# A chunked TTT scan and an FFN on one core: the scan's step planned in branches, its state in one PSUM tile, the weight guard on GpSimd

## The chip, the cores and the metric

The kernel runs on one core of a Trainium2 chip. The metric is the device time of one execution in microseconds. Three executions of the kernel before took 1038.76, 1048.29 and 1051.76 us; their median is 1048.29 us. The profile is of a further execution.

Five engines appear in it: PE (TensorE, matmuls; PEld is its loading of weights), DVE (VectorE), ACT (ScalarE), POOL (GpSimd) and SP (SyncE, which here only issues DMAs). Each runs its own instructions in the order in which the program holds them, and waits on semaphores of the others.

## The reference, cut to what matters

The input is x, 2048 rows of 512. The first layer projects its normalised rows to q, k, v (16 heads of 32 columns) and beta, and runs a scan over chunks of 16 rows:

```python
def step(S, inp):
    qi, ki, vi, ei = inp
    kh = einsum('bchd,bhde->bche', ki, S)
    target = vi - ki
    mu, rstd = mean(kh), rsqrt(var(kh) + EPS)
    kh_hat = (kh - mu) * rstd
    gw = (w * kh_hat + b - target) * w
    v_new = (gw - mean(gw) - kh_hat * mean(gw * kh_hat)) * rstd
    A = where(tri, einsum('bchd,bshd->bhcs', qi, ki), 0) * ei
    qh = einsum('bchd,bhde->bche', qi, S) - einsum('bhcs,bshe->bche', A, v_new)
    o = qi + _ln(qh, w, b)
    S = S - einsum('bchd,bche->bhde', ki * ei, v_new)
    return (S, o)
```

There are 128 such steps, and each needs the state S of the one before. A gate, a norm and a projection by Wo follow. The second layer is an FFN with 512 to 1536 to 512 columns, whose three weights are rounded to float8 (e4m3fn, as float32 values) before use, so that values beyond 448 become NaN.

## The kernel before

**The parts.** The rows are worked in 16 blocks of 128, each of 8 steps. For each block `pre` normalises, turns and projects the rows, and lays k out in `kb` and, by way of DRAM, in `kr`; `gram` forms the products of k with the k of the step before; `pre_v` makes the target rows; `pre_sig` makes q and the gate; `scores` and `post` make the output of a block that the scan has left. `weights` rounds the FFN's weights in 36 parts of 128 x 512 while the scan runs: DVE makes a magic number m per value (L1067, L1070), POOL adds and subtracts it (L1074, L1076), ACT makes a guard that is 0, or NaN beyond 448 (L1080, L1082), and POOL adds it (L1087). The FFN starts when the scan has ended.

**One step of the scan** (`chain`), with the names that the prediction uses:

1. DVE: the first product (L901) and the second (L906) of kh with prepared rows, then sums over the columns (L929).
2. ACT: the state S is copied from PSUM, in two operations, one for each of the two banks `ups[0]` and `ups[1]` (L916). PE: kS, the next step's k times that S, into the bank of kh (L877).
3. ACT: a root (L933). DVE: the reciprocal iv (L936), y (L939), k1 (L943), k2 (L951), sk (L953), kk (L956), and the product m (L959).
4. ACT: u, two operations (L946), from a row and k1.
5. DVE: u plus m (L969), and vb (L972), the new values.
6. PE: Gv (L990) adds gram times vb to kh, which completes the next step's kh; and up (L1002) adds the step's k times vb to the state, in PSUM.

The state, the small numbers and u share two PSUM banks, each a tile of its own: `ups[0]` holds half the state and `nums` (iv, y, kk), `ups[1]` the other half and u:

```python
ups = [p_up.tile([P, D], F32, tag=f"up{j}", name=f"up{j}")[:, 0:128] for j in range(2)]
nums, u = ups[0], ups[1][:, 64:128].rearrange("p (r e) -> p r e", r=2)
```

What must wait for what is found by the framework from the tiles that an instruction reads and writes; the kernel states none of it.

**The order.** A planner written into the kernel (`Sched`) sets each engine's order when the program is built. All work is tasks that ask for an engine for so many microseconds. The planner always places the operation that can start first, by its own durations (the table `steps` for a step of the scan, `TENSOR` for PE, with a switch cost `SWITCH` and a preference `SAME` for work of the same array shape). Tasks marked `chain` announce when they will need each engine (`need`); other work goes in front only if it ends no later than that plus `SLACK`. On PE, matmuls whose result nobody reads (`spare`, 128 x 384, named "none") are placed where less than `SPARE` of work lies in the last 3.4 us, and a shorter filler goes into kh's bank ahead of Gv (L982). The whole step is one task, `chain`, which asks for its operations one after the other. At a block's border the wait for the next block's `kb` and its kS stand before the sum of step 5.

Of the kernel before, what the change touches and what calls it, by code (L numbers as in the profile page):

```python
# [9 lines left out]
F32 = mybir.dt.float32  # L10
F32R = mybir.dt.float32r
I32 = mybir.dt.int32
AF = mybir.ActivationFunctionType
ALU = mybir.AluOpType
# [47 lines left out]

SPARE, SPARE_OVER, SPARE_GAP = 1.3, 0.1, 0.3
SWITCH, SAME = 0.1, 0.25
TENSOR = {
# [27 lines left out]
class Sched:  # L95
# [2 lines left out]

    SLACK = {"PE": 0.3, "DVE": 0.3, "ACT": 0.35, "POOL": 0.0, "SP": 0.0}

    def __init__(self):
        self.engine = {"PE": 0.0, "DVE": 0.0, "ACT": 0.0, "POOL": 0.0, "SP": 0.0}
# [77 lines left out]
    def run(self):  # L182
        while True:
            self._settle()
            ops = [t for t in self.tasks if t["req"][0] == "op"]
            if not ops:
                assert not self.tasks, [t["gen"].__name__ for t in self.tasks]
                return
            need = {}
            for t in ops:  # L190
                if t["chain"]:
                    at = self._start(t)
                    need[t["req"][1]] = at
                    for eng, after in (t["req"][3] or {}).items():
                        need.setdefault(eng, at + after)
            best = None
            for eng in self.engine:
                mine = [(self._start(t), t) for t in ops if t["req"][1] == eng]
                fit = [
                    (s, t) for s, t in mine  # L200
                    if t["chain"] or eng not in need or s + self._us(t) <= need[eng] + self.SLACK[eng] + t["req"][6]
                ]
                fit = [(s, t) for s, t in fit if t["req"][5] != "spare" or self._spare(s, t, mine, need.get(eng))]
                if not fit:
                    continue
                first = min(s for s, _ in fit)
                s, t = min(((s, t) for s, t in fit if s <= first + 1e-9), key=lambda x: self._rank(x[1]))
                if best is None or s < best[0]:
                    best = (s, t)
            s, t = best  # L210
            eng, dur = t["req"][1], self._us(t)
            if eng == "PE":
                _, self.part, work = TENSOR[t["req"][5]]
                self.idle = s - self.engine[eng]
                self.array.append((s, work))
            else:
                self.table = t["req"][5] or self.table
            self.engine[eng] = s + dur
            self.now = max(self.now, s)
            t["ready"] = s + dur + t["req"][4]  # L220
            t["last"] = eng
            self._advance(t, t["ready"])
# [11 lines left out]
def kernel(  # L234
# [79 lines left out]
    with ExitStack() as st1:  # L314
# [63 lines left out]
        kh_bank = p_kh.tile([P, D], F32, tag="kh", name="kh")  # L378
        kh = kh_bank[:, 0 : 2 * DH].rearrange("p (r e) -> p r e", r=2)

        ups = [p_up.tile([P, D], F32, tag=f"up{j}", name=f"up{j}")[:, 0:128] for j in range(2)]

        nums, u = ups[0], ups[1][:, 64:128].rearrange("p (r e) -> p r e", r=2)
        iv, y = nums[:, 64:66], nums[:, 66:74].rearrange("p (s r) -> p s r", r=2)
# [58 lines left out]
        def norm_row(src, tag, newton=False):  # L443

            yield op("DVE", 0.73)
            st = small.tile([P, 6], F32, tag=tag + "st", name="st")
            nc.vector.bn_stats(st, src)
            yield op("DVE", 0.18)
            mv = small.tile([P, 2], F32, tag=tag + "mv", name="mv")
            nc.vector.bn_aggr(mv, st)  # L450
            if newton:
                r = yield from rsqrt_parts(mv[:, 1:2], [P, 1], 1.0, 1e-5, small, tag + "n")
            else:
                yield ("take", tables, 1)
                end = yield op("ACT", 0.3, table="sqrt")
                z = small.tile([P, 1], F32, tag=tag + "z", name="z")
                act(z, mv[:, 1:2], AF.Sqrt, bias=eps5)
                tables.put(end)
                yield op("DVE", 0.4)
                r = small.tile([P, 1], F32, tag=tag + "r", name="r")  # L460
                nc.vector.reciprocal(r, z)
            nb = small.tile([P, 1], F32, tag=tag + "nb", name="nb")
            stt(nb, mv[:, 0:1], -1.0, r, ALU.mult, ALU.mult)
            return r, nb
# [307 lines left out]
        def post(b):  # L772
# [76 lines left out]


        steps = [
            ("DVE", 0.4, 0.0), ("DVE", 0.33, 0.4), ("ACT", 0.42, 0.32), ("PE", "kS", 0.86), ("DVE", 0.47, 0.73),
            ("ACT", 0.28, 1.32), ("DVE", 0.2, 1.2), ("DVE", 0.2, 1.4), ("DVE", 0.2, 1.6), ("ACT", 0.8, 1.92),
            ("DVE", 0.2, 1.8), ("DVE", 0.2, 2.0), ("DVE", 0.2, 2.2), ("DVE", 0.33, 2.4), ("DVE", 0.26, 2.84),
            ("DVE", 0.23, 3.1), ("PE", "Gv", 3.45, 0.2), ("PE", "up", 3.8, 0.22),
# [3 lines left out]
        def chain_ops():  # L859
            out = []  # L860
            for n, (eng, us, at, *late) in enumerate(steps):
                need = {}
                for m in range(1, len(steps) + 1):
                    e, _, start, *_ = steps[(n + m) % len(steps)]
                    need.setdefault(e, start - at + (period if n + m >= len(steps) else 0.0))
                need.pop(eng, None)
                late = late[0] if late else 0.0
                if eng == "PE":
                    out.append(pe(us, need, late))
                else:  # L870
                    out.append(op(eng, us, need, late, "sqrt" if (eng, us) == ("ACT", 0.28) else None))
            return out

        def k_S(b, i, S, stop):
            for g in range(4):
                half = slice(64 * (g % 2), 64 * (g % 2) + 64)
                nc.tensor.matmul(  # L877
                    kh[half, g // 2, :], lhsT=kbs[b % 2][:, i, g, :], rhs=S[:, g, :], start=(g < 2), stop=stop and g > 1,
                )

        def chain():
            ops = chain_ops()
# [4 lines left out]
            for b in range(NB):  # L887
                if b >= 2:
                    yield ("wait", at_out[b - 2])
                for i in range(NC):  # L890
# [16 lines left out]
                        row[:, :, 6:8, 0:DH], kh.unsqueeze(2).to_broadcast([P, 2, 2, DH]), row[:, :, 3:5, 0:DH],  # L907
                        ALU.mult,
                    )
                    op_S = next(step)  # L910
                    if b or i:
                        yield ("at", t_up + HOP)
                        yield op_S
                        S = state.tile([P, 4, DH], F32, tag="S" if i else "S0", name="S")
                        for j in range(2):
                            nc.scalar.copy(S[:, j:4:2, :], ups[j][:, 0 : 2 * DH].rearrange("p (r e) -> p r e", r=2))  # L916
                    if i == 0:
                        data[b]["S"] = S
                    op_K = next(step)
                    if not end:  # L920
                        nb, ni = (b, i + 1) if i + 1 < NC else (b + 1, 0)
                        n2 = 2 * nb + ni // NHALF
                        if ni:
                            yield ("wait", ready[nb])
                            yield op_K
                            k_S(nb, ni, S, False)
                    yield ("at", t0)
                    t0 = yield next(step)
                    nc.vector.tensor_reduce(z[:, 0:4, :].rearrange("p s r -> p r s"), row[:, :, 4:8, :], AX.X, ALU.add)  # L929
                    t1 = yield next(step)  # L930

                    sk = small.tile([P, 2, 2], F32, tag="sk", name="sk")
                    act(sk[:, 0, :], z[:, 2, :], AF.Sqrt)  # L933
                    yield ("at", t0)
                    yield next(step)
                    nc.vector.reciprocal(iv, z[:, 2, :])  # L936
                    yield next(step)
# [3 lines left out]

                    k1 = small.tile([P, 2, 2], F32, tag="k1", name="k1")
                    stt(k1, z[:, 0:6:5, :], -1.0 / DH, y[:, 3:4, :].to_broadcast([P, 2, 2]), ALU.mult, ALU.mult)  # L943
                    t3 = yield next(step)
                    for r in range(2):
                        act(u[:, r, :], row[:, r, 4, 0:DH], AF.Identity, bias=k1[:, 0, r : r + 1], scale=k1[:, 1, r : r + 1])  # L946
                    yield ("at", max(t1 + HOP, t2))
                    yield next(step)

                    k2 = small.tile([P, 2], F32, tag="k2", name="k2")  # L950
# [9 lines left out]
                        m, row[:, :, 2:4, 0:DH],  # L960
                        kk.rearrange("p s r -> p r s").unsqueeze(3).to_broadcast([P, 2, 2, DH]), ALU.mult,
                    )
                    if not end and ni == 0:
                        yield ("wait", ready[nb])
                        yield pe("kS")
                        k_S(nb, ni, S, False)
                    yield ("at", max(t3 + HOP, t4))
                    yield next(step)
                    tt(u, m[:, :, 0, :], u, ALU.add)  # L969
                    t5 = yield next(step)  # L970
# [2 lines left out]
                    sched.add(give(b, i, vb), rank=-4)  # L973
                    if end:
                        break
                    yield ("wait", gram_in[n2])
                    t_kh = yield next(step)
                    work, idle = sched.array_work()
# [76 lines left out]
        def one_part(f, part, raw, loaded, before, marks):  # L1055
# [6 lines left out]
            yield ("at", loaded)  # L1062
            yield from turn(0)
            yield ("take", ms, 1)
            yield op("DVE", 0.6)
            m = rnd.tile([P, D], F32, tag="m", name="m")
            ts(m.bitcast(I32), raw.bitcast(I32), 0x7F800000, None, ALU.bitwise_and)  # L1067
            marks[0].set(0.0)
            yield op("DVE", 0.6)
            ts(m, m, 2.0**-6, 1.5 * 2.0**20, ALU.max, ALU.mult)  # L1070
            yield from turn(1)
            yield op("POOL", 1.35)
# [3 lines left out]
            gtt(v, v, m, ALU.subtract)  # L1076
            marks[1].set(0.0)

            yield op("ACT", 0.65)
            act(m, v, AF.Copy, scale=1.1 * 2.0**119)  # L1080
            yield op("ACT", 0.65)
            act(m, m, AF.Copy, scale=0.0)  # L1082
            yield from turn(2)
            yield ("take", ws, 1)
            end = yield op("POOL", 1.35)
# [304 lines left out]
```

## Time and profile before

| what | value |
| --- | --- |
| runs | 1038.76, 1048.29, 1051.76 us (median 1048.29) |
| the profiled execution's own time | 1042.52 us |
| its span, first to last instruction | 1040.7 us |
| granted TensorE clock, mean | 0.971 |
| first product of the scan, first and last | 45.7 and 728.8 us |
| PE "none" matmuls (L1021) | 125, 106.1 us busy |
| ACT u (L946) | 256 operations, 0.381 us each |
| ACT copies of the state (L916) | 254 operations, 0.214 us each |
| ACT guard (L1080, L1082) | 72 operations, 45.2 us |
| POOL busy | 513.4 us |

The span falls into 45.7 us up to the first step, 683 us of scan, and the rest, which is FFN with the last blocks' output beside it. A matmul of this kernel in float32 leaves two records, which is why PE's counts are twice the program's. In the lists "idle before" is the time that the engine stood still ahead of an operation, and the name behind the arrow is what ended it. A table by stage gives for each engine the busy time, with the number of records in brackets, and then the granted clock, the share of the DMA engines and GB/s.

### The profile page before, as it was taken

Reading aid. Unit: us, or ns where it says so; the run is one execution under the profiler, and the core shown is the slowest. Engines: PE = TensorE matmul, PEld = TensorE weight load, DVE = VectorE, ACT = ScalarE, POOL = GpSimd, SP = SyncE. Lnnn points to the kernel's source line nnn. Section 1 sums busy time; section 2 is a strip of 40 time slices with the busy share of each in tenths; the row PEclk is TensorE's granted clock in tenths of the full one; section 3 lists DMA queues with packets and bytes.
Section 4 is the critical chain, followed back from the end, with each engine's and each line's share of the span. In section 5 each row is a group of like instructions: output and inputs, shape, how many; then the busy total and the mean of one; then the engine's idle time right before and its main releaser. Section 6 shows DMA issues by size and latency. Waiting matters only on the chain.

```text
span 1040.7 us, 22812 instructions
## 1 busy us (share of the span) xinstructions
PE 977.6 (94%) x8150; PEld 651.2 (63%) x8150; DVE 681.2 (65%) x2291; ACT 535.4 (51%) x1373; POOL 513.4 (49%) x476
## 2 busy tenths in 40 slices
PE   4899999999998899999999999999799999999996
PEld 2456665656654565555656556556467888888885
DVE  3267777778688468777675757656565476665635
ACT  1556756666666456674665657654332232232223
POOL 4648578778467587668375887533420010010001
PEclk9999999999899999999999999999899999999998
DMA  9423323324223222222313232232204000010001
GB/s 294 132 57 83 92 53 80 69 76 104 69 49 85 67 44 70 65 70 64 72 30 83 67 78 70 49 92 66 74 1 182 1 31 11 1 41 0 11 31 41
DMA packets 139393, 69.08 MB, mean 66 GB/s; under 512 B 106640, under 2 KB 119056, under 8 KB 139280
## 3 DMA queue, kind: packets, MB, share of 16 engines
q1 hardware_dynamic: 138256, 66.35, 24.2%
q8 instruction: 65, 1.06, 0.5%
q0 software_dynamic: 272, 0.87, 0.3%
q10 hardware_dynamic: 752, 0.40, 0.2%
q14 instruction: 48, 0.39, 0.1%
HBM read 41.25 MB, written 26.35 MB: 65 GB/s over the span
## 4 chain that ended last, share of the span: by engine, by line
PE 74%; DVE 11%; ACT 6%; DMA 3%; POOL 3%; issue 2%; SPq 0%; ACTq 0%; DVEq 0%; POOLq 0%
PE gu L1189 17%; PE acc L1218 8%; PE pk L487 5%; PE none L1021 5%; PE po L487 5%; PE pq L708 5%; PE up L1002 5%; PE pv L487 5%; PE kh L990 4%; PE kh L877 3%; PE pr L570 3%; PE pt L472 2%; ACT up L946 2%; DMA wv_s<-in_wv_dram 1%; PE qh L792 1%
## 5 line engine op out<-in xcount | busy, mean ns | idle before, releaser
L1189 PE MATMUL gu<-xh,w 128*128 128x512 f32 x384 | 152.4, 397 | 2.8 <-DVE sg L1237 2.1
L1189 PE MATMUL gu<-xl,w 128*128 128x512 f32 x384 | 151.5, 394 | 0.0
L1291 POOL TENSOR_TENSOR y<-y,xa 128x512 f32<-128x512 f32 x15 | 19.3, 1288 | 226.2 <-ACT y L1285 226.2
L946 ACT ACTIVATE up<-row,k 128x32 f32<-128x32 f32 x256 | 97.7, 381 | 51.3 <-DVE k L951 41.9
L1021 PE MATMUL none<-lwb,cs 128*128 128x384 f32 x250 | 106.1, 538 | 7.5 <-DVE q L728 2.6
L901 DVE TENSOR_TENSOR row<-kh,row 128x192 f32<-128x192 f32 x128 | 45.7, 357 | 86.8 <-PE kh L990 79.9
L1218 PE MATMUL acc<-w,h 128*128 128x512 f32 x384 | 97.0, 395 | 0.4 <-DVE h L1248 0.2
L768 POOL TENSOR_TENSOR at<-at,cs 128x512 f32<-128x512 f32 x64 | 81.4, 1299 | 24.4 <-ACT at L761 24.1
L916 ACT COPY S<-up 128x64 f32<-128x64 f32 x254 | 41.3, 214 | 84.9 <-PE up L1002 84.2
L1189 PEld LDWEIGHTS gu<-xh,w 128*128 128x128 f32 x384 | 72.9, 190 | 19.0 <-DVE sg L1237 2.8
L1002 PE MATMUL up<-vb,kr 64*128 64x32 f32 x1016 | 83.7, 279 | 0.0
L877 PEld LDWEIGHTS kh<-S,kb 128*64 128x64 f32 x1016 | 42.6, 139 | 65.2 <-ACT S L916 22.9
L1218 PEld LDWEIGHTS acc<-w,h 128*128 128x128 f32 x384 | 72.5, 190 | 16.6 <-ACT h L1246 0.6
L1189 PEld LDWEIGHTS gu<-xl,w 128*128 128x128 f32 x384 | 72.9, 190 | 15.4 <-DVE xl L1170 0.4
L990 PEld LDWEIGHTS kh<-vb,gram 64*64 64x64 f32 x1016 | 39.7, 134 | 60.8 <-DVE vb L972 31.7
L1087 POOL TENSOR_TENSOR w<-raw,m 128x512 fp32r<-128x512 f32 x36 | 45.9, 1274 | 61.4 <-DMA w8d<-w 24.5
L1246 ACT CAST h<-sg 128x512 fp32r<-128x512 f32 x48 | 29.9, 622 | 88.0 <-DVE sg L1240 74.9
L1002 PEld LDWEIGHTS up<-vb,kr 64*128 64x128 f32 x1016 | 69.6, 188 | 7.3 <-issue 2.6
L487 PE MATMUL pv<-wv_s,xt 128*128 128x512 f32 x128 | 66.2, 629 | 2.8 <-ACT xt L475 2.3
L487 PE MATMUL po<-wo_s,ot 128*128 128x512 f32 x128 | 67.7, 641 | 0.0
L487 PE MATMUL pk<-wk_s,xt 128*128 128x512 f32 x128 | 66.8, 640 | 0.0
L708 PE MATMUL pq<-wq_s,xt 128*128 128x512 f32 x128 | 66.5, 637 | 0.0
(197 smaller groups left out, 2098.9 us busy)
## 6 DMA issues: line engine op xcount, KB each, us to landing
w8d<-w SPq DMA_DIRECT2D x36, 256.0 KB
w<-w8d SPq DMA_DIRECT2D x12, 768.0 KB
tg_d<-tg SPq DMA_DIRECT2D x32, 132.0 KB
row<-tg_d SPq DMA_DIRECT2D x32, 132.0 KB
kc_d<-kn SPq DMA_DIRECT2D x16, 256.0 KB
kr<-kc_d SPq DMA_DIRECT2D x256, 16.0 KB
vb_d<-vb SPq DMA_DIRECT2D x128, 32.0 KB
vbt<-vb_d SPq DMA_DIRECT2D x16, 256.0 KB
```

What stands on the lines that cost most here:

```text
L487: nc.tensor.matmul(pp, lhsT=lhs[:, k, :], rhs=rhs[:, k, :], start=(k == 0), stop=(k == 3))
L708: nc.tensor.matmul(pq, lhsT=xt[:, k, :], rhs=wq_s[:, k, :], start=(k == 0), stop=(k == 3))
L768: gtt(view, view, causal.unsqueeze(1).to_broadcast([P, 4, P]), ALU.mult)
L877: nc.tensor.matmul(kh[half, g // 2, :], lhsT=kbs[b % 2][:, i, g, :], rhs=S[:, g, :], start=(g < 2), stop=stop and g > 1,)
L901: tt(row[:, :, 3:6, 0:DH], kh.unsqueeze(2).to_broadcast([P, 2, 3, DH]), row[:, :, 0:3, 0:DH], ALU.mult,)
L946: act(u[:, r, :], row[:, r, 4, 0:DH], AF.Identity, bias=k1[:, 0, r : r + 1], scale=k1[:, 1, r : r + 1])
L990: nc.tensor.matmul(kh[half, r, :], lhsT=grams[n2 % 2][half, ni % NHALF, r, :], rhs=vb[half, r, :], start=False, stop=(r == 1),)
L1002: nc.tensor.matmul(ups[j][:, r * DH : r * DH + DH], lhsT=kr[half, ii, r, :], rhs=vb[half, r, :], start=(b == 0 and i == 0 and r == 0), sto ...
L1021: nc.tensor.matmul(none[:, 0:384], lhsT=ident, rhs=lwb[:, 0:384], start=True, stop=True)
L1087: gtt(w, v, m, ALU.add)
L1189: nc.tensor.matmul(pp, lhsT=w[:, half, k * P : (k + 1) * P], rhs=part[:, k, :], start=(k == 0 and i == 0), stop=(k == 3 and i == 1),)
L1218: nc.tensor.matmul(accs[tb][s], lhsT=h[:, i, s * P : (s + 1) * P], rhs=w8[f][:, 2, :], start=(f == 0 and i == 0), stop=(f == NF - 1 and i ...
```

## The change

The two banks become one tile, and the two copies of the state one operation over both. The step is planned in branches: `older` (the copy of the state and kS), `on_act` for the root and for u, and the vector operations in `chain`, which waits for events of the others. The wait for the next block's `kb` moves into `older`. The guard becomes one GpSimd operation with two multiplications. Numbers of the planner change with it: `SPARE`, `SAME`, the slack of PE, some durations, and how the needs are kept.

```diff
-SPARE, SPARE_OVER, SPARE_GAP = 1.3, 0.1, 0.3
-SWITCH, SAME = 0.1, 0.25
+SPARE, SPARE_OVER, SPARE_GAP = 1.6, 0.1, 0.3
+SWITCH, SAME = 0.1, 0.0
...
-    SLACK = {"PE": 0.3, "DVE": 0.3, "ACT": 0.35, "POOL": 0.0, "SP": 0.0}
+    SLACK = {"PE": 1.0, "DVE": 0.3, "ACT": 0.35, "POOL": 0.0, "SP": 0.0}
...
-                    need[t["req"][1]] = at
-                    for eng, after in (t["req"][3] or {}).items():
-                        need.setdefault(eng, at + after)
+                    for eng, after in {t["req"][1]: 0.0, **(t["req"][3] or {})}.items():
+                        need[eng] = min(need.get(eng, at + after), at + after)
...
-        ups = [p_up.tile([P, D], F32, tag=f"up{j}", name=f"up{j}")[:, 0:128] for j in range(2)]
+        up_banks = p_up.tile([P, 2, D], F32, tag="up", name="up")
+        ups = [up_banks[:, j, 0:128] for j in range(2)]
...
-            ("DVE", 0.4, 0.0), ("DVE", 0.33, 0.4), ("ACT", 0.42, 0.32), ("PE", "kS", 0.86), ("DVE", 0.47, 0.73),
+            ("DVE", 0.4, 0.0), ("DVE", 0.33, 0.4), ("ACT", 0.28, 0.32), ("PE", "kS", 0.72), ("DVE", 0.47, 0.73),
...
+                if eng == "ACT" or n == 3:
+                    need = {"PE": 0.4} if n == 2 else {}
...
+        def older(b, i, after, t_up, S, old, op_S, op_K):
+
+            if b or i:
+                yield ("at", t_up + HOP)
+                yield op_S
+                S = state.tile([P, 4, DH], F32, tag="S" if i else "S0", name="S")
+                nc.scalar.copy(
+                    S.rearrange("p (r j) e -> p j r e", j=2), up_banks[:, :, 0 : 2 * DH].rearrange("p j (r e) -> p j r e", r=2),
+                )
+            if i == 0:
+                data[b]["S"] = S
+            if after is None:
+                return
+            nb, ni = after
+            yield ("wait", ready[nb])
+            t = yield op_K
+            k_S(nb, ni, S, False)
+            old.set(t)
+
+        def on_act(what, done, at, emit):
+            yield ("at", at + HOP)
+            t = yield what
+            emit()
+            done.set(t + HOP)
+
+        def values(row, k1):
+
+            for r in range(2):
+                act(u[:, r, :], row[:, r, 4, 0:DH], AF.Identity, bias=k1[:, 0, r : r + 1], scale=k1[:, 1, r : r + 1])
...
-                    op_S = next(step)
-                    if b or i:
-                        yield ("at", t_up + HOP)
-                        yield op_S
-                        S = state.tile([P, 4, DH], F32, tag="S" if i else "S0", name="S")
-                        for j in range(2):
-                            nc.scalar.copy(S[:, j:4:2, :], ups[j][:, 0 : 2 * DH].rearrange("p (r e) -> p r e", r=2))
...
+                    sched.add(
+                        older(b, i, None if end else (nb, ni), t_up, S, old, next(step), next(step)), rank=-9, chain=True,
+                    )
...
+                    root, part = Event(), Event()
+                    sched.add(on_act(next(step), root, t0, lambda: act(sk[:, 0, :], z[:, 2, :], AF.Sqrt)), rank=-9, chain=True)
...
-                    t3 = yield next(step)
-                    for r in range(2):
-                        act(u[:, r, :], row[:, r, 4, 0:DH], AF.Identity, bias=k1[:, 0, r : r + 1], scale=k1[:, 1, r : r + 1])
-                    yield ("at", max(t1 + HOP, t2))
+                    sched.add(on_act(next(step), part, t2, lambda: values(row, k1)), rank=-9, chain=True)
+                    yield ("wait", root)
...
-                    if not end and ni == 0:
-                        yield ("wait", ready[nb])
-                        yield pe("kS")
-                        k_S(nb, ni, S, False)
-                    yield ("at", max(t3 + HOP, t4))
+                    yield ("wait", part)
...
+                    yield ("wait", old)
                     yield ("wait", gram_in[n2])
...
-            yield op("ACT", 0.65)
-            act(m, v, AF.Copy, scale=1.1 * 2.0**119)
-            yield op("ACT", 0.65)
-            act(m, m, AF.Copy, scale=0.0)
+            yield op("POOL", 1.4)
+            nc.gpsimd.tensor_scalar(m, v, 1.1 * 2.0**119, 0.0, ALU.mult, ALU.mult)
```

Left out are three planned durations on DVE (a reciprocal 0.4 to 0.6, the two operations on m 0.6 to 0.82 and 0.72).

More of the change, by code (lines that the diff above doesn't have):

```diff
@@ L458, in norm_row @@
                 tables.put(end)
-                yield op("DVE", 0.4)
+                yield op("DVE", 0.6)
                 r = small.tile([P, 1], F32, tag=tag + "r", name="r")
@@ L909, in chain @@
                     )
-                    op_S = next(step)
-                    if b or i:
-                        yield ("at", t_up + HOP)
-                        yield op_S
-                        S = state.tile([P, 4, DH], F32, tag="S" if i else "S0", name="S")
-                        for j in range(2):
[L916 to L919, printed above, removed]
+                    old = Event()
                     if not end:
@@ L922, in chain @@
                         n2 = 2 * nb + ni // NHALF
-                        if ni:
-                            yield ("wait", ready[nb])
-                            yield op_K
-                            k_S(nb, ni, S, False)
-                    yield ("at", t0)
+                    sched.add(
+                        older(b, i, None if end else (nb, ni), t_up, S, old, next(step), next(step)), rank=-9, chain=True,
+                    )
                     t0 = yield next(step)
                     nc.vector.tensor_reduce(z[:, 0:4, :].rearrange("p s r -> p r s"), row[:, :, 4:8, :], AX.X, ALU.add)
-                    t1 = yield next(step)
                     sk = small.tile([P, 2, 2], F32, tag="sk", name="sk")
-                    act(sk[:, 0, :], z[:, 2, :], AF.Sqrt)
-                    yield ("at", t0)
+                    root, part = Event(), Event()
+                    sched.add(on_act(next(step), root, t0, lambda: act(sk[:, 0, :], z[:, 2, :], AF.Sqrt)), rank=-9, chain=True)
                     yield next(step)
@@ L962, in chain @@
                     )
-                    if not end and ni == 0:
-                        yield ("wait", ready[nb])
-                        yield pe("kS")
-                        k_S(nb, ni, S, False)
-                    yield ("at", max(t3 + HOP, t4))
+                    yield ("wait", part)
                     yield next(step)
@@ L1064, in one_part @@
             yield ("take", ms, 1)
-            yield op("DVE", 0.6)
+            yield op("DVE", 0.82)
             m = rnd.tile([P, D], F32, tag="m", name="m")
@@ L1068, in one_part @@
             marks[0].set(0.0)
-            yield op("DVE", 0.6)
+            yield op("DVE", 0.72)
             ts(m, m, 2.0**-6, 1.5 * 2.0**20, ALU.max, ALU.mult)
```

## The prediction

> **What bounds the kernel now.** I read the engine line first, then a table by stage, then one step of the scan in the timeline, then the waits. The engine line of the page:
>
> ```profile
> PE 977.6 (94%) x8150; PEld 651.2 (63%) x8150; DVE 681.2 (65%) x2291; ACT 535.4 (51%) x1373; POOL 513.4 (49%) x476
> ```
>
> PE looks full everywhere, but part of that is the filler "none" (106.1 us), so the share says little. By stage (us, then busy us of PE, PEld, DVE, ACT, POOL, then the granted clock):
>
> ```profile
> 246.40:287.00 40.60, 39.32 (x418) 24.68 (x417) 28.29 (x113) 25.66 (x73) 23.62 (x23) 0.92 0.33 84
> 693.90:729.00 35.10, 32.72 (x380) 21.14 (x379) 21.79 (x91) 19.46 (x57) 10.51 (x9) 0.90 0.29 90
> 45.70:729.00 683.30, 654.74 (x6743) 402.44 (x6744) 487.97 (x1870) 426.07 (x1193) 447.91 (x417) 0.97 0.29 70
> 745.00:1040.70 295.70, 283.75 (x1294) 229.14 (x1292) 168.72 (x352) 88.78 (x140) 28.83 (x22) 0.97 0.08 31
> ```
>
> The scan's 128 steps take 683 us; the FFN behind them 296 us, where PE alone is the limit. The change touches the scan. One step there is 5.38 us on average, 4.81 in the median, 3.72 at the least. What a step consists of on DVE, and the one ACT line beside it:
>
> ```profile
> 303.88 0.17 DVE L936 RECIPROCAL up<-z 128x2 f32<-128x2 f32 x1
> 304.09 0.17 DVE L939 TENSOR_TENSOR up<-z,up 128x8 f32<-128x8 f32 x1
> 304.29 0.16 DVE L943 SCALAR_TENSOR_TENSOR k<-z,up 128x4 f32<-128x4 f32 x1
> 304.37 0.15 DVE L951 TENSOR_TENSOR k<-up,sk 128x2 f32<-128x2 f32 x1
> 304.55 0.80 ACT L946 ACTIVATE up<-row,k 128x32 f32<-128x32 f32 x2 [0.53 <-DVE k L951]
> 304.56 0.16 DVE L953 SCALAR_TENSOR_TENSOR sk<-up,k 128x2 f32<-128x2 f32 x1
> 304.75 0.17 DVE L956 TENSOR_TENSOR up<-sk,up 128x4 f32<-128x4 f32 x1
> 304.95 0.29 DVE L959 TENSOR_TENSOR m<-row,up 128x128 f32<-128x128 f32 x1
> 305.37 0.23 DVE L969 TENSOR_TENSOR up<-m,up 128x64 f32<-128x64 f32 x1
> 305.64 0.22 DVE L972 TENSOR_TENSOR vb<-m,up 128x64 f32<-128x64 f32 x1
> ```
>
> See that ACT's pair (u, 0.80 us) runs beside four DVE operations (k2, sk, kk, m) and ends 0.02 us before the sum that needs it. It costs almost nothing today. The waits say who is late (us in total, times, longest):
>
> ```profile
> DVE row L901 <- PE kh L990: 79.9, 84, 6.0
> DVE up L936 <- ACT S L916: 16.8, 12, 3.5
> ```
>
> In 84 of 128 steps DVE waits for PE's kh product. So a step is the larger of two lengths. **Length D**, the vector branch: first product to end of vb 3.20 us, then 0.05 to PE and 0.47 to the next first product, 3.72 together, plus filler operations that the order puts between, and those behind vb beyond 0.52. **Length P**, PE's work in its fixed order: 1.29 for kS, Gv and up, plus all filler between them, plus at least 0.5 between up and kS while the state is copied. Filler prices from the chain and the gaps between matmul records: 0.93 a wide product (4 records 1.91), 0.70 a "none" (6 records 2.13), 0.5 a turn, 1.15 a half of gram. Taking the larger, step by step for steps 1 to 126, gives 650 us; the trace has 678. P is the larger in 71 steps, D in 55. Of the 28 left, about 20 are the clock: 0.97 over 683 us is 3% lost, in stretches such as the two with 0.92 and 0.90.
>
> **The change part by part.**
>
> *One tile of two banks: a wait is added.* This decides my forecast. The built program's waits show it: in the kernel before, k2, sk and kk wait on nothing of u, since `nums` and u lie in two tiles. After, all lie in one tile, and every DVE operation that touches `up` is ordered against ACT's u, although no byte is shared. In 65 steps u waits for k2 and sk waits for u; in 31 k2 itself waits for u; in 31 u waits for kk and m waits for u; in 1 kk waits. In each case the 0.80 us pair no longer lies beside the vector operations but between them. Worked out for the first case on the rows above: u 304.62 to 305.42, then sk, kk, m, the sum and vb at today's spacings (0.19, 0.20, 0.33, 0.27, 0.22), end 306.65 instead of 305.86: +0.79. The second gives +0.91, the third +0.80. I take 0.80. Behind the waiting operation stand on DVE the rest of the step, then Gv on PE, then everything. The bounds are 0 (PE is later anyway) and 0.91.
>
> The Trainium skill, "PSUM — Partial Sum Buffer", section "PSUM bank collisions raise a hardware error", holds that engines must be kept apart by bank and quadrant and that accesses to different banks run clean. By that rule u (second bank) and `nums` (first) need no order, the wait would be worth nothing and the sum would be the 1046 of the first rival; but the built program holds the waits whether the chip needs them or not, and no run here shows the chip without them.
>
> *The steps in branches, and the planner's numbers.* Only the order changes; the counts on DVE and SP stay. I priced PE's new order as above. PE's own work is the same: P alone sums to 626 us against 621 (9 more "none", 6.3 us; 2240 fewer columns of kh filler, 3.8 us less). DVE filler behind the second product falls from 47 us to under 1, behind vb it rises from 83 to 135. PE work between Gv and up rises from 9 to 52 us (45 steps hold a wide product or its like); it delays up, the copy of the state and the reciprocal L936, which waits for that copy: from Gv 1.34 + B to the reciprocal, where it has 1.68 free, so 0.6 late when B is 0.93. All in, without the wait on u: 654 us, +4. With 0.80 on D: **711, +61**. D or that copy's path then decides in 100 of 126 steps instead of 55.
>
> *One copy for the state.* Today two COPY of 0.214, overlapping to 0.31 to 0.33. One of 128 elements: between 0.204 (128x8, L645) and 0.586 (128x512), nearest 0.257 (64x128, L662). Some 0.06 less in 127 steps: 8 us of ACT, worth 0 to 8; I take 0, because PE's filler stands after up anyway. In 27 or so steps the copy and the root stand in front of u on ACT, behind k1: +0.45 there, 12 us, half of it where D decides: +6.
>
> *The guard.* ACT loses 72 operations, 45.2 us (L1080, L1082). POOL gains 36: the nearest row is L352, the same kind and size, 1.55 us; the low end is L620's 0.25 at 128x16. At 1.55 that is 56 us on an engine that idles 235 of the scan's 683. The last part is written at step 107, and beyond the first loads the weights are wanted at the scan's end: that covers it. Without the cover, one such operation ahead of the masks or of kb at each of 15 block borders costs 23 us; ACT's relief can give back at most its 45. I take 0.
>
> The row of L1070 on DVE runs from 0.415 to 1.532 us with a median of 0.846, the short ones where POOL rests. The skill's "GPSIMD Engine Reference", section "1. Specifications", has GpSimd and VectorE share an SBUF interface, contended by VectorE's two-port modes, which speaks against this edit: 36 more holds of up to 1.1 us, an estimate of 0 to 40 us on DVE by page and row. I leave it out of the sum, because that filler now stands behind vb.
>
> **The sum.** +61 by the two lengths, +6 for late copies, and -13 for the clock: half-clock stretches cost where P decides, 20 x 26/71 leaves 7. Together +54. The profiled execution took 1042.52 us (span 1040.7); it lies 5.8 below the median of the runs, 1048.29. 1042.5 + 54 = **1096**. About 2% is what a measurement of this kernel can tell from no change (the runs spread over 1.2%).
>
> **Rivals.**
>
> *PE hides the wait (14%).* If my PE prices are low, P decides nearly every step and u's wait falls into PE's shadow: +4, 1046. For it: PE is busy 655 of 683 us. Against: 106 us of that is "none", and DVE waits for kh only 80 us in all, 0.6 per step, less than 0.8.
>
> *Faster: full clock and clean order (7%).* The threshold for "none" rises (1.3 to 1.6), so the clock could stay at full rate, and the filler that stood inside the vector branch is gone. The place is the scan; the price the whole 28 us above my sum. With +4: 1018. It decides only if u's wait is hidden in nearly every step; at 0.8 us, 57 us stand against 28.
>
> *Borders (13%).* PE's order still holds two blocks of filler before a block's first product: 17.8 us ahead of step 63's kS and 12.4 ahead of step 96's (before: 17.0 and 13.8 at 55 and 103; the first of these took 29.0 us, 8 more than its work). With a busier POOL such borders lose 10 to 15 us each: 1122.
>
> *The edit does not do what it says:* the branches exist in the planner, but the waits tie them together; that is the forecast itself. The one copy and the one GpSimd operation are there.
>
> **How the numbers follow.** Forecast 66%, own range 1070 to 1125; rivals 14, 7, 13%. Left out below 1045: the faster case and half of the first rival; the top takes in the borders: 1045 to 1130. Faster by over 2% 7%; within 2% the first rival and 3 from the forecast, 17%; slower 76%.
>
> **What will show it.** In the new profile, the row of k2, sk and m should carry idle time put down to ACT's u of some 0.5 us or more per step, 50 us in all; the shortest step should be near 4.5 instead of 3.72; DVE's wait for kh should fall well under 80 us; the span from 745 on should keep its 296 us. A shortest step near 3.7 would prove me wrong at the root; a shortest step of 4.5 with an unchanged scan would mean PE hid it. What else could spoil it: the low clock in more stretches than today, since PE rests longer in each step.

## The result, and the profile after

The kernel after takes 1093.88 us (median of four runs, 1093.19 to 1097.39); the kernel before, on the same chip, 1045.49 us. The ratio is **1.047, 95% interval 1.040 to 1.055**: slower by 48 us, with 1096 forecast. The profiled execution took 1097.39 us (span 1095.4).

The engine line of the page after (us busy, share of the span, instructions):

```profile
PE 1005.8 (92%) x8140; PEld 657.4 (60%) x8140; DVE 685.0 (63%) x2291; ACT 490.6 (45%) x1174; POOL 535.4 (49%) x512
```

ACT has 45 us less to do and DVE nearly the same, in a span 55 us longer. The table by stage has, for each engine, the busy time with its records in brackets, then the granted clock, DMA share and GB/s:

```profile
45.80:782.20 736.40, 684.52 (x6684) 408.79 (x6686) 493.71 (x1870) 381.79 (x994) 469.23 (x452) 0.94 0.27 65
798.00:1095.40 297.40, 283.16 (x1296) 229.12 (x1296) 170.97 (x357) 90.69 (x144) 30.06 (x23) 0.98 0.08 31
```

The scan takes 736 us in place of 683; the part behind it, 297 us, is about as long as before (296). The time came in inside the scan's steps: the median step grew from 4.81 to 5.31 us and the shortest from 3.72 to 4.46. One step in the timeline (start, length, engine, line, what ended the idle time before it):

```profile
215.10 0.16 DVE L963 SCALAR_TENSOR_TENSOR k<-z,up 128x4 f32<-128x4 f32 x1
215.17 0.15 DVE L969 TENSOR_TENSOR k<-up,sk 128x2 f32<-128x2 f32 x1
...
215.36 0.80 ACT L911 ACTIVATE up<-row,k 128x32 f32<-128x32 f32 x2 [0.56 <-DVE k L969]
...
216.19 0.16 DVE L971 SCALAR_TENSOR_TENSOR sk<-up,k 128x2 f32<-128x2 f32 x1 [0.86 <-ACT up L911]
216.38 0.17 DVE L974 TENSOR_TENSOR up<-sk,up 128x4 f32<-128x4 f32 x1
216.59 0.29 DVE L977 TENSOR_TENSOR m<-row,up 128x128 f32<-128x128 f32 x1
```

k2 (L969) ends at 215.32, u starts 0.04 us later, and sk (L971) starts 0.03 us after u's end, though it reads nothing of u. The 0.80 us pair that stood beside sk, kk and m now stands alone between k2 and sk. Over the whole run, from the waits (us in total, times, longest):

```profile
DVE sk L971 <- ACT up L911: 56.9, 64, 2.1
DVE row L933 <- PE kh L1005: 45.9, 44, 10.1
...
DVE m L977 <- ACT up L911: 28.6, 31, 0.9
...
DVE k L969 <- ACT up L911: 23.9, 27, 1.4
```

With one of 1.0 us at kk, DVE waits **110.4 us for u in 123 of 128 steps**; before it was 4.0, all of it at the sum that needs u. The wait for PE's kh fell from 79.9 to 45.9 us. The chain of work that ended last, by engine, shows the shift from PE (74% before) to DVE (11% before):

```profile
PE 60%; DVE 19%; ACT 7%; DMA 4%; issue 4%; POOL 3%; SPq 1%; ACTq 0%; DVEq 0%; POOLq 0%
```

### The profile page after: what moved, and what is told of

Its sections match the earlier page's. It is cut to its first block, busy times and chain, and to the rows that moved or that the text cites. A ratio compares the mean times of both kernels' runs of the same rounds, so it can differ in the third digit from the quotient of the medians.

```text
span 1095.4 us, 22396 instructions
## 1 busy us (share of the span) xinstructions
PE 1005.8 (92%) x8140; PEld 657.4 (60%) x8140; DVE 685.0 (63%) x2291; ACT 490.6 (45%) x1174; POOL 535.4 (49%) x512
## 4 chain that ended last, share of the span: by engine, by line
PE 60%; DVE 19%; ACT 7%; DMA 4%; issue 4%; POOL 3%; SPq 1%; ACTq 0%; DVEq 0%; POOLq 0%
PE gu L1202 16%; PE acc L1231 8%; PE none L1036 5%; ACT up L911 5%; PE up L1017 4%; PE pq L708 4%; PE pk L487 4%; PE po L487 4%; PE kh L1005 3%; PE pv L487 3%; PE kh L879 2%; PE pt L472 2%; DVE m L977 2%; DMA wo_s<-in_wo_dram 1%; PE qh L799 1%
## 5 line engine op out<-in xcount | busy, mean ns | idle before, releaser
L1036 PE MATMUL none<-lwb,cs 128*128 128x384 f32 x268 | 118.9, 556 | 1.6 <-ACT gram L577 0.7
L1005 PE MATMUL kh<-vb,gram 64*64 64x32 f32 x1016 | 54.8, 228 | 34.7 <-DVE vb L986 32.3
L889 ACT COPY S<-up 128x128 f32<-128x128 f32 x127 | 33.6, 264 | 115.1 <-PE up L1017 82.2
L933 DVE TENSOR_TENSOR row<-kh,row 128x192 f32<-128x192 f32 x128 | 45.2, 353 | 59.2 <-PE kh L1005 45.9
L708 PE MATMUL pq<-wq_s,xt 128*128 128x512 f32 x128 | 71.8, 683 | 0.0
L1259 ACT CAST h<-sg 128x512 fp32r<-128x512 f32 x48 | 29.9, 623 | 88.1 <-DVE sg L1253 74.9
```

Of the source, the lines that this page charges most:

```text
L708: nc.tensor.matmul(pq, lhsT=xt[:, k, :], rhs=wq_s[:, k, :], start=(k == 0), stop=(k == 3))
L889: nc.scalar.copy(S.rearrange("p (r j) e -> p j r e", j=2), up_banks[:, :, 0 : 2 * DH].rearrange("p j (r e) -> p j r e", r=2),)
L933: tt(row[:, :, 3:6, 0:DH], kh.unsqueeze(2).to_broadcast([P, 2, 3, DH]), row[:, :, 0:3, 0:DH], ALU.mult,)
L1005: nc.tensor.matmul(kh[half, r, :], lhsT=grams[n2 % 2][half, ni % NHALF, r, :], rhs=vb[half, r, :], start=False, stop=(r == 1),)
L1036: nc.tensor.matmul(none[:, 0:384], lhsT=ident, rhs=lwb[:, 0:384], start=True, stop=True)
```

## The experiments

The theory (A): the framework orders u against DVE's small operations because both lie in the one tile, and that costs the time. The main rival (B): it is the new order, the guard on GpSimd or the block borders. All ratios are to the kernel before, run beside.

### Two tiles again, and one tile alone

The kernel after, with two tiles and two copies. Fewer than 20 of DVE's 2291 instructions change places, and beside the second copy none of ACT's or POOL's:

```diff
-        up_banks = p_up.tile([P, 2, D], F32, tag="up", name="up")
-        ups = [up_banks[:, j, 0:128] for j in range(2)]
+        ups = [p_up.tile([P, D], F32, tag=f"up{j}", name=f"up{j}")[:, 0:128] for j in range(2)]
...
-                nc.scalar.copy(
-                    S.rearrange("p (r j) e -> p j r e", j=2), up_banks[:, :, 0 : 2 * DH].rearrange("p j (r e) -> p j r e", r=2),
-                )
+                for j in range(2):
+                    nc.scalar.copy(S[:, j:4:2, :], ups[j][:, 0 : 2 * DH].rearrange("p (r e) -> p r e", r=2))
```

> The kernel after, with the state's sums again in two tiles of one bank each and copied by two ScalarE operations; the branches, the planner's numbers and the guard on GpSimd stay, and the planned order stays but for a few swaps on VectorE. Theory A (u, ordered against VectorE's small operations by the shared tile, costs some 50 us): the idle time of sk, k2, m and kk that is put on u falls from 110 us to under 10, the shortest step returns to about 3.7 us, and the time to about 1046 us (1030 to 1062). Theory B (the new order, the guard on GpSimd or the borders of blocks cost it): 1080 to 1100 us.

Measured: **1045.07 us**, ratio 1.007 (1.004 to 1.010), as A had it. Its DVE waits:

```profile
DVE row L931 <- PE kh L1003: 75.1, 82, 9.2
...
DVE up L981 <- ACT up L909: 3.7, 6, 1.0
```

No small operation waits for u any more; only the sum that needs it (L981) does, 3.7 us in all. The shortest step is 3.75 us. And the reverse edit, made in the kernel before and nothing else:

> The kernel before, with only the one tile of two banks and the single copy of the state; no branches, old planner numbers, guard on ScalarE as before. Theory A: k2 now waits for u in all 128 steps, the idle time put on u is 80 to 120 us, the shortest step is 4.4 us or more, and the time 1085 to 1110 us. Theory B: 1038 to 1052 us, as before, or a little less for the saved copies.

Measured: **1106.88 us**, ratio 1.065 (1.060 to 1.071), 69 us above the kernel before, and the shortest step 4.63 us:

```profile
DVE k L953 <- ACT up L948: 118.7, 124, 4.0
DVE sg L1239 <- ACT sg L1236: 42.6, 27, 2.3
DVE row L902 <- PE kh L992: 41.3, 50, 4.8
```

In the old order u is written into the program ahead of k2, so k2 itself waits, nearly a microsecond each in 124 steps. Taking the one tile out removes most of the loss, and putting it in, in another order, makes one. B falls as the main cause.

### u in a place of its own, with one tile and one copy kept

Is it u, or the single copy over two banks? First, u alone in SBUF:

```diff
-        state = st1.enter_context(tc.tile_pool(name="state", bufs=3))
+        state = st1.enter_context(tc.tile_pool(name="state", bufs=2))
...
-        nums, u = ups[0], ups[1][:, 64:128].rearrange("p (r e) -> p r e", r=2)
+        nums = ups[0]
+        u = w1.tile([P, 2, DH], F32, tag="u_own", name="u_own")
```

> The kernel after, with u in a tile of its own in SBUF, so that the two banks hold only the sums of the state and the small numbers; two buffers of the state in place of three make the room. The single copy, the branches, the planner's numbers and the guard on GpSimd stay. Theory A: as with two tiles, 1030 to 1062 us, with the idle time put on u under 10 us; below the run with two tiles by what the single copy is worth, 0 to 10 us. If the one copy or the one tile costs by another way than u (copy against the small numbers in the same tile), the time stays 15 us or more above the run with two tiles. Theory B: 1080 to 1100 us.

Measured: **1091.25 us**, ratio 1.052 (1.046 to 1.058): the time that B named, but not for a reason of B. The wait on u is gone (4.2 us are left, of the sum that needs it), and the shortest step is 3.72 us. So my range for A was missed by 29 us, by something neither theory had. The groups of lines (busy us and mean ns behind the bar) show what took its place:

```profile
L987 DVE TENSOR_TENSOR vb<-m,u_own 128x64 f32<-128x64 f32 x128 | 77.2, 603 | 4.8 <-DVE u_own L984 0.5
...
L984 DVE TENSOR_TENSOR u_own<-m,u_own 128x64 f32<-128x64 f32 x128 | 59.8, 467 | 12.3 <-ACT u_own L912 4.2
```

In the kernel after the same two adds, with u in PSUM:

```profile
L983 DVE TENSOR_TENSOR up<-m,up 128x64 f32<-128x64 f32 x128 | 28.5, 222 | 2.8
L986 DVE TENSOR_TENSOR vb<-m,up 128x64 f32<-128x64 f32 x128 | 28.2, 221 | 4.6 <-DVE up L983 0.2
```

(467 - 222) + (603 - 221) = 627 ns a step, 80 us in 128, at the end of DVE's part where Gv waits. The timeline of that run shows one such add:

```profile
219.90 1.26 POOL L614 TENSOR_TENSOR u<-lbb,u 128x512 f32<-128x512 f32 x1
...
220.06 1.19 DVE L984 TENSOR_TENSOR u_own<-m,u_own 128x64 f32<-128x64 f32 x1 [0.17 <-ACT u_own L912]
...
221.28 0.23 DVE L987 TENSOR_TENSOR vb<-m,u_own 128x64 f32<-128x64 f32 x1
```

The add of 0.23 us begins under a GpSimd operation (POOL) and ends 0.09 us after it. So do the other long ones: of the 128 adds of each line 53 and 58 take over 0.3 us, all of them begin under a GpSimd operation, and 110 of the 111 end 0.07 to 0.09 us after that operation's end (the last one after the end of the next). Of the 145 short ones 29 begin under one, in its last 0.21 us. The guard on GpSimd, which B names, makes 4.5 of the 101.5 us that the long adds lie under GpSimd; the rest is other work. "SBUF — State Buffer" of the Trainium skill, section "🔬 SBUF: two separate sides", states it: a VectorE operation with two SBUF inputs and a GpSimd operation that reads SBUF share one pair of ports, and whichever starts first holds it for the whole instruction. The run agrees: an add of 0.23 us was held for up to 1.1 us. In the kernel after, where u lies in PSUM, 124 of the 256 adds lie wholly under a GpSimd operation, and none took more than 0.230 us.

So the next run keeps one operand of each add in PSUM, by putting m there:

```diff
+        m_all = up_banks[:, 1, 128:256].rearrange("p (r s e) -> p r s e", r=2, s=2)
...
-                    m = sc.tile([P, 2, 2, DH], F32, tag="m", name="m")
+                    m = m_all
```

> The kernel after with u in a tile of its own in SBUF, and m, which was in SBUF, in columns 128 to 255 of the second bank of the sums; three buffers of the state. In the run with u alone in SBUF the two adds that end VectorE's part of a step, with both operands then in SBUF, took 467 and 603 ns in the mean, not 222 and 221, the long ones nearly all under a GpSimd operation. Here each add has one operand in PSUM. Theory A (the order of u against the small numbers is what the change costs, and that run was slow for the adds alone): adds of 0.21 to 0.25 us, idle time put on u under 10 us, 1035 to 1052 us. Theory C (the single copy of two banks, or one tile for the sums and the small numbers, costs it by another way than u): 1075 us or more with short adds.

Measured: **1044.94 us**, ratio 1.0045 (1.002 to 1.007), as with two tiles:

```profile
L988 DVE TENSOR_TENSOR vb<-up,u_own 128x64 f32<-128x64 f32 x128 | 28.7, 224 | 5.0 <-DVE u_own L985 0.5 <-DMA kr<-kc_d 0.2
L985 DVE TENSOR_TENSOR u_own<-up,u_own 128x64 f32<-128x64 f32 x128 | 28.7, 224 | 12.5 <-ACT u_own L913 4.2
```

Both adds are back at 224 ns, and PE's Gv, which waited 30.6 us for vb in the former run, waits 6.6. The one tile with its single copy costs nothing that shows once u lies elsewhere, and that the held adds made the former run's 1091 us is shown by taking them away. The state's buffers changed too (two there, three here), but in the former run no idle time of the copy is put down to a reader of an older S: 101.8 us of it end with up and 22 with results of DVE. A gain of the single copy does not show either: the intervals of 1.0045 and 1.007 overlap.

### The guard, and the planner's figure for it

These runs take up what else B holds, the guard and the planned order. The kernel after with the guard back on ScalarE:

```diff
-            yield op("POOL", 1.4)
-            nc.gpsimd.tensor_scalar(m, v, 1.1 * 2.0**119, 0.0, ALU.mult, ALU.mult)
+            yield op("ACT", 0.65)
+            act(m, v, AF.Copy, scale=1.1 * 2.0**119)
+            yield op("ACT", 0.65)
+            act(m, m, AF.Copy, scale=0.0)
```

> The kernel after, with the weights' guard again as two ScalarE operations, planned as before; the one tile, the single copy and the branches stay. Theory A: 1085 to 1105 us, little changed, for the wait on u stays. Theory B, in the form that the guard on GpSimd costs it (36 operations there): under 1065 us.

Measured: 1106.48 us, ratio 1.064 (1.059 to 1.069), with 105 us of waits for u, just above A's range. It is no better without GpSimd's guard, rather 13 to 17 us worse (by the times and by the ratios), in an order in which over a thousand of DVE's instructions stand elsewhere. The same edit beside two tiles:

> The kernel of the run with two tiles (branches, planner's numbers, two copies), with the guard back as two ScalarE operations. It leaves of the change the branches and the planner's numbers alone. If the guard on GpSimd saves in the scan what it saves with one tile (1094 against 1106 us), 1052 to 1062 us; if it is the guard that put the run with two tiles at 1045 against 1038 us of the kernel before, 1030 to 1042 us; if it does neither, 1043 to 1050 us.

Measured: 1050.67 us, ratio 1.011 (1.008 to 1.014), between the ranges. The branches and the planner's figures alone cost 12 us against the kernel before, and the guard on GpSimd, in the run with two tiles, gives 4 to 6 of them back. The guard alone, put into the kernel before:

> The kernel before with the guard alone moved to GpSimd as one operation, planned at 0.65 us, near the 0.62 us that it took. If the 36 operations of 0.6 us on GpSimd come cheaper than 72 of ScalarE, 1022 to 1034 us; if it does nothing, 1035 to 1046 us; if it delays VectorE's operations on SBUF as GpSimd's operations did in the run with u in SBUF, 1046 us or more.

Measured: 1067.07 us, ratio 1.027 (1.023 to 1.030): the third range, but not for its reason, as the next run's figures show. Planned at 1.4 us:

> The kernel before with the guard on GpSimd, planned at 1.4 us, as the kernel after plans it, in place of 0.65 (which took 1067 us). The operations are the same, so what differs is the planned order alone. If GpSimd's guard itself slows VectorE or the queue of GpSimd in this kernel, 1060 to 1075 us again; if the order decides, some other time, most likely 1035 to 1055 us.

Measured: 1062.35 us, ratio 1.021 (1.015 to 1.028). With the step as it was, the same 36 operations lose 23 to 28 us, planned at 0.65 or at 1.4. The planner makes another order for each of the two, and neither is that of the kernel before, so that the guard's own cost and that of the order are not told apart. It is not a delay of the step's own DVE operations by GpSimd: the twelve of a step sum to 2.78 us in each of the two profiles (mean lengths; 2.78 before), and DVE's whole busy time in the scan is 491.65 us in the first, 487.97 before. In the first of them the steps are 20 us longer in all even when none is counted above 8 us, and what the few long ones take beyond that is 14 us more; the part behind the scan is 9 us shorter. In one stall of 25.4 us, at step 95, the chain that ended last shows kb's copies on POOL behind a row of other operations. Whether that is the cause of the whole was not tried and stays open.

GpSimd's guard takes 0.617 us in the median, not 1.4. In the run with two tiles, the planner told 0.65:

```diff
-            yield op("POOL", 1.4)
+            yield op("POOL", 0.65)
```

> The kernel of the run with two tiles, with the guard on GpSimd planned at 0.65 us in place of 1.4, so that the planner's order follows the 0.62 us that it took. If the planner's wrong figure costs, 1030 to 1041 us; if the order around it does not matter, 1041 to 1050 us.

Measured: **1026.55 us**, ratio 0.988 (0.985 to 0.992), below the range. Scan and end are both shorter, by 6 and 12 us; step 63, 29.9 us in the run with two tiles and 30.3 in the kernel after, is among the normal ones, though steps 71, 103 and 119 take 12 to 22 and step 81 8.9. What steps take above 8 us fell from 31 to 25 us. The same figure, with one tile, u in SBUF and m in PSUM, and then in the kernel after as it is:

> The run with u in SBUF and m in the second bank (one tile, single copy, branches, guard on GpSimd), with the guard planned at 0.65 us in place of 1.4. With two tiles the same figure took 1045 to 1027 us, by the stalls at the borders of blocks (step 63: 29.9 us to none over 8) and a shorter end. If the order is set by the planned figures alone, the same here: 1020 to 1032 us, faster than both kernels; if the figure's gain was luck of one run of the planner with two copies, 1038 to 1050 us.

> The kernel after as it is, with only the guard's planned time at 0.65 us. Theory A: the wait on u stays (about 110 us of idle time put on u, shortest step 4.4 us or more), and the plan's gain of some 18 us is had beside it: 1070 to 1085 us, some 45 to 55 us over the same order with u apart. If the wait on u matters only in the order as it was, under 1050 us.

Measured: **1026.05 us**, ratio 0.987 (0.981 to 0.993), and **1075.10 us**, ratio 1.034 (1.027 to 1.041), side by side on one chip, both within their ranges. The DVE waits of the second:

```profile
DVE sk L971 <- ACT up L911: 62.5, 72, 0.9
...
DVE row L933 <- PE kh L1005: 28.5, 33, 3.9
...
DVE m L977 <- ACT up L911: 21.4, 23, 1.1
...
DVE k L969 <- ACT up L911: 16.7, 23, 0.9
```

With 3.8 at kk that is 104.4 us on u; in the first only the sum that needs u waits for it, 1.5 us. The orders of the two differ in fewer than ten of DVE's instructions and in none of ACT's or POOL's, so the pair prices the order of u at **49 us**, under a plan whose borders differ from those of the kernel after. The first of the pair beats the kernel before by 1.3% and the kernel after by more; it has all of the change's parts, with u and m moved and the guard's time corrected. But the run with two tiles, this one and the kernel after have one order but for a few of DVE's instructions, and the same three with 0.65 another one: the 18 us are one plan against one plan, seen three times. That such a gain is luck of the plan is not excluded, and in the kernel before 0.65 did no better than 1.4 (1067.07 against 1062.35 us).

## Why the prediction was right

**The added wait: right in place, mechanism and size of one.** Of the 123 steps with a wait, 0.90 us each on average, where 0.79 to 0.91 was worked out. The shortest step is 4.46 us for the 4.5 named, and 0.75 above the one before; in the run where k2 waits in nearly every step it is 4.63, the +0.91 that was worked out for that form. The idle time on sk, m and k2 is there in the three forms and nearly the counts (64, 31 and 27 for 65, 31 and 31). Two readings were slightly off: in the rows shown u (304.55) starts after k2 has ended (304.52), so it stood beside three operations and not four; and the working let u start at 304.62, without which the first case comes to +0.72.

**Its price: somewhat too high.** Of the +61 us of the two lengths 4 are the order's and 57 the wait's. The pair above has 49; the kernel after against the run with u in SBUF and m in PSUM, 1.0471 / 1.0045, has some 44, and against the run with two tiles, 1.0471 / 1.0068, some 42. In "the larger of two lengths" more of the wait was covered than the priced lengths said; which price was off was not traced. DVE idles 242.7 us of the scan after (736.40 less 493.71) and 183.1 in the run without the wait, whose stage line is

```profile
45.50:731.50 686.00, 661.38 (x6686) 397.22 (x6688) 502.89 (x1870) 370.61 (x995) 469.98 (x452) 0.97 0.29 69
```

so that 110 us of waits made 60 us of idle time: DVE's wait for kh gave 26 back (72.1 to 45.9), smaller gaps the rest. The rival that PE hides the wait was right in part.

**The order itself, +4 on the steps, and late copies, +6.** Together with the guard, the run with two tiles shows +7 (1.004 to 1.010), near the two together (+10), but made up otherwise: branches and figures cost 12 and the guard saves 4 to 6. The late copies are there: in 22 steps (27 or so were counted) the copy stands on ACT between k1 and u, and u starts 0.57 us after k1's end in the mean, where the median before is 0.10; that is 10 us, where 12 was worked out. How much of it reaches the time, half by the prediction, no run shows. One figure does not add up: 9 more "none" less the shorter kh filler make 2.5 us, not the 5 by which P grew.

**The clock, -13: not borne out.** The sum let the loss to the low clock fall from about 20 us to 7. But the scan's granted clock fell from 0.97 to 0.94: a loss of at most 44 us (6% of 736) in place of 20 (3% of 683). How much of it reached the time no run shows; the prediction let it cost only where PE decides. The low clock goes with the wait: the scan's mean is lower with u's wait than in the same order without it, 0.94 against 0.97 (two tiles, and u and m moved), and 0.98 against 0.99 in the later pair. It is lower also in the run whose adds were held, 0.95. The stretch from 356 to 372 us of the kernel after, where PE waits 2.0 us ahead of one kS, has 0.68. That PE's rests are the cause was not tried. The prediction named this as what could spoil it, and counted the other way. The fall to 0.94 is not needed for the loss, for the later pair has 49 us at 0.98 and 0.99.

**So the sum came near in part by luck.** The wait was priced 8 to 15 us too dear. All the rest was taken at -3 (+4, +6 and -13) and measured +5 to +7, by the two runs without the wait. The two errors go against each other.

**The guard at 1.55 us, worth nothing: mis-sized.** It takes 0.617 us, 22.5 us in all and not 56 (shortest, median and longest in ns, in the profile after):

```profile
L1095 POOL TENSOR_SCALAR m<-raw x36: 610/617/882, 71.7 to 659.2; 128x512 f32<-128x512 f32 x36
```

The row used for it was not like it: that line multiplies by a number per partition, 1.552 us in the profile after too, where the guard multiplies by constants. Nor is it worth nothing: with the order that the planner then made, moving it to GpSimd changed the time by -24 us (two tiles, 1050.67 to 1026.55) and by +28 (the kernel before), and why is known only in part.

**The single copy, worth nothing: right.** It takes 0.266 us in the median (0.257 taken).

**The bank rule** of the Trainium skill, "PSUM — Partial Sum Buffer", section "PSUM bank collisions raise a hardware error", by which accesses to different banks need no order, had made 1046 of a kernel without the wait. u with the same banks but two tiles, and so without the wait, took 1045.07: the rule and the run agree, and the lost time was the framework's caution, not the chip's need.

**The rivals.** Borders: step 63 did stall for 30.3 us, as its 17.8 us of filler let one expect, but the kernel before has one of 29.0 at step 55; what the steps take above 8 us sums to 34 us after and 38 before. They explain nothing of this change. In the runs with the planner told 0.65 the scan, borders among it, gave some 6 us and the shorter end 12. The faster case failed at its condition, that the wait be hidden in nearly every step.

## What to carry to other kernels

In these kernels a tile is the grain at which the framework orders work: joining two tiles to save one instruction put ACT's u in order with DVE's operations on the other half. The price is the operation that used to run beside the others, once per step, less what was covered (0.80 us of 128 steps is 102 us, and 42 to 49 of it came through; 69 in the old order). Read the built program's waits before and after, and where an operand is moved to break such an order, ask which port it then shares. In a planned kernel, measure an operation before you plan with it: here the figure nearer to the measured one (0.65 for 1.4) made a plan 18 us shorter, though in the kernel before it made none.

## What the hardware showed that I had not expected

- A 0.23 us VectorE add with both inputs in SBUF took up to 1.33 us when it began under a GpSimd operation, 0.467 and 0.603 us in the mean of 128, and ended some 0.08 us after that operation; with one input in PSUM it never took more than 0.230.
- GpSimd's multiplication of 128 x 512 by two constants took 0.617 us, by one number per partition 1.552 us.
- One ScalarE copy of 128 elements over two PSUM banks took 0.266 us, where two of half the size had taken 0.214 each.
